# A selective scan's next chunk, prepared at other places of the loop: TensorE's fills, ScalarE's activations and one product moved

## The chip, the cores and the metric

The kernel runs on one NeuronCore of a Trainium2 chip. Five engines work side by side: TensorE (PE in the profile; its weight loads are PEld), VectorE (DVE), ScalarE (ACT), GpSimd (POOL), and SyncE (SP), which here only issues transfers. Each engine executes its own instructions in the order in which the program gives them, and semaphores tie the engines together. The metric is the device time of one execution, in microseconds (us).

## The reference, cut to what matters

Four layers are applied in turn to four images of 256 channels on 64 x 64 places: a deformable convolution, an attention layer, a second deformable layer, and a state-space layer (Mamba). The change touches the last of them alone. With `_gn` a group normalisation over 32 groups, `xs` the 4096 places of an image as a sequence, it computes

```
xz = xs @ in_proj_w.T;  u, res = split(xz)            # 512 channels each
u = silu(causal_conv4(u) + conv_b)                    # four taps per channel
dt, Bm, Cm = split(u @ x_proj_w.T)                    # 16, 16, 16
delta = softplus(dt @ dt_proj_w.T + dt_proj_b)        # 512 channels
state = exp(delta * A) * state + delta * Bm * u       # 16 states per channel, over the sequence
y = sum over states of state * Cm;  y = (y + u * D) * silu(res)
x = x + y @ out_proj_w.T
```

## The kernel before, in words

**Tiling.** Everything is float32 but the weights that repeat a row of B. The 512 channels are four blocks `dc` of 128 partitions. The sequence of an image is cut into 8 chunks of 512 places, and a chunk has 16 steps, one for each state n. So the loop in `layer3` runs over 128 steps s for each of four images; chunk j = s // 16, n = s % 16.

**One step.** TensorE repeats row n of B over all partitions into a PSUM bank, `bn` (`state`, L1460; there is one such bank). VectorE multiplies du = delta * u with it (L1537: 2048 elements per partition, or 1536 at the eight "helped" n, 14, 15 and 0 to 5, where GpSimd makes the fourth block at L1468 from a copy of the row that a transfer brought, `bs`). Then, for each of the four blocks, ScalarE makes da = exp(delta * A) (L1547, into one of two PSUM banks) and VectorE runs the scan over it (L1548). GpSimd keeps the last column (`carry`, L1560) and multiplies with the repeated row of C (L1563; `cn`, a transfer, four buffers). Two steps later TensorE adds the four blocks into PSUM with an identity matrix (`add`, L1438; called y below). `h` has four buffers. At n = 2 VectorE gates the four sums of the chunk before (`gated`, L1514).

**The preparation of the next chunk** (`front`) and the output projection of the last (`close`) are cut into small parts, and a table `slots` puts each part at a place: a step and a half. A part has up to two functions: `pe`, which issues TensorE's matmuls into the one bank `front`, and `rest`, which empties the bank by ScalarE, or does other work. `fill(s, half)` issues the first matmul part of a place ahead of time; `empty(s, half)` issues the rests, and further matmul parts. Half 0 is emptied after the second scan of a step and half 1 after the fourth; half 2 follows GpSimd's product; half -1 is ahead of the scans. The parts of chunk j > 1 begin LEAD steps ahead of their base: step 0 of `front(j)` falls on n = 16 - LEAD of chunk j - 2, that is, most of the preparation for chunk k + 1 runs during chunk k.

The parts: `begin` (two activations of 512 that normalise the chunk); four projections, P0 to P3 (L1242, each four matmul rows of the profile); four convolutions, C0 to C3 (L1285, eight rows); the silu over all blocks with a second one for the gate, and a load of an activation table ahead of each change of function; shares (dt, B, C; L1309) and their eviction; four steps of the delta projection (L1324) with two activations each; Exp, "one" (1 + exp), its complement (L1351), Ln, each an activation of 2048; three additions and one product on GpSimd; three copies in bf16 that split the rows of B exactly (`split`); four gate projections (also L1242). `close` has two output products Z0, Z1 (L1396 and L1400, ten rows each), each followed by an eviction and a transfer out; `fetch` loads the next image's chunk; `count` has VectorE's statistics of it (L152).

**What sets the order.** Under `manual_schedule` TensorE, ScalarE, VectorE and GpSimd execute in the order in which this loop is written. In step s TensorE has: the bank of half 0 (filled at the end of the step before), the fill of half 1, `bn` of step s + 1, the y of step s - 2. At each place ScalarE has the parts in the order in which they were put.

Of the kernel before, what the change touches and what calls it, by code (L numbers as in the profile page):

```python
# [9 lines left out]
F32 = mybir.dt.float32  # L10
# [6 lines left out]
P = 128  # L17
# [46 lines left out]
class Net:  # L64
# [1016 lines left out]
    def layer3(self, x, out, nxt, early):  # L1081
# [3 lines left out]

        nc, tc = self.nc, self.tc
        C = 512
        NC, LEAD = N // C, 4  # L1090
        with (
            tc.tile_pool(name="l3a", bufs=1) as pa,
            tc.tile_pool(name="l3b", bufs=2) as pb,
# [23 lines left out]
            nc.gpsimd.memset(carry, 0.0)  # L1117
            tail = pa.tile([P, 4, 3], F32, tag="tail", name="tail")
            nc.gpsimd.memset(tail, 0.0)
            kept = pa.tile([P, 2, C], F32, tag="kept", name="kept")  # L1120
            chunks = [{} for _ in range(NC)]

            def bank():
# [112 lines left out]
            def project(j, dc, to):  # L1236
                c = chunks[j]

                def pe():
                    c["b"] = bank()  # L1240
                    for ct in range(2):
                        nc.tensor.matmul(  # L1242
                            c["b"], win[:, ct, bass.ts(dc, P)], c["xn"][:, ct, :], start=(ct == 0), stop=(ct == 1)
                        )

                return pe, lambda: nc.scalar.copy(to(), c["b"])

            def gate(j, dc):
                def to():
                    if dc == 0:  # L1250
                        chunks[j]["sres"] = pb.tile([P, 4, C], F32, tag="sres", name="sres")
                    return chunks[j]["sres"][:, dc, :]

                return project(j, 4 + dc, to)
# [5 lines left out]
            def front(j):  # L1260
# [15 lines left out]
                put(0, 0, None, begin)  # L1276

                for dc in range(4):
                    put((dc + 1) // 2, (dc + 1) % 2, *project(j, dc, lambda dc=dc: c["up"][:, dc, 3:]))

                def convolve(dc):
                    def pe():
                        c["b"] = bank()
                        for i in range(4):
                            nc.tensor.matmul(  # L1285
                                c["b"], conv[:, dc, i, :], c["up"][:, dc, i : i + C], start=(i == 0), stop=(i == 3)
                            )

                    def rest():
                        nc.scalar.activation(c["u"][:, dc, :], c["b"], AF.Identity, bias=cb[:, dc : dc + 1])  # L1290
                        if dc == 0:
                            nc.gpsimd.tensor_copy(tail, c["up"][:, :, C : C + 3])

                    return pe, rest

                for dc in range(4):
                    put(2 + dc, 1, *convolve(dc))
                def silu():
                    nc.scalar.activation(c["u"], c["u"], AF.Silu)
                    gate_silu(j - 1)  # L1300
                    tables()

                put(6, 0, None, silu)

                def shares():

# [8 lines left out]
                    c["cd"] = self.dram.tile([2 * DS, C], F32, tag="cd", name="cd")  # L1315
                    nc.sync.dma_start(out=c["cd"], in_=c["dbc"][16:48, :])

                put(7, 1, shares, keep)


                def step(dc):
# [11 lines left out]
                    return pe, rest  # L1333

                for dc in range(4):
                    put(8 + dc // 2, dc % 2, *step(dc))
                put(10, 0, None, lambda: nc.scalar.activation(c["du"], c["du"], AF.Exp, scale=-1.0))

                def one():
                    c["w"] = pa.tile([P, 4, C], F32, tag="w3", name="w3")  # L1340
                    nc.scalar.activation(c["w"], c["du"], AF.Identity, bias=self.ones[:, 0:1])

                put(10, 1, None, one)


                put(10, 2, None, lambda: nc.gpsimd.tensor_add(c["delta"], c["delta"], c["du"]))
                put(
                    12,
                    0,
                    None,  # L1350
                    lambda: nc.scalar.activation(c["du"], c["w"], AF.Identity, bias=self.ones[:, 0:1], scale=-1.0),  # L1351
                )
                put(13, 0, None, lambda: nc.scalar.activation(c["w"], c["w"], AF.Ln))
                last = 17 if j > 1 else 15
                put(13, 2, None, lambda: nc.gpsimd.tensor_add(c["delta"], c["delta"], c["du"]))
                put((13 + last) // 2, 2, None, lambda: nc.gpsimd.tensor_add(c["delta"], c["delta"], c["w"]))
                put(last, 2, None, lambda: nc.gpsimd.tensor_mul(c["du"], c["delta"], c["u"]))

                for dc in range(4):
                    at = ((14, 0), (14, 1), (15, 0), (15, 1)) if j > 1 else ((10, 1), (11, 0), (11, 1), (12, 1))  # L1360
                    put(*at[dc], *gate(j, dc))
                def split(i):
                    def part():
                        if i == 0:
# [14 lines left out]
                    return part  # L1379

                for i in range(3):
                    put((11, 12, 14)[i], i % 2, None, split(i))
                return todo

            def close(j):

                c = chunks[j]
                last = j == NC - 1
                todo = []

                def project(ot):
                    def pe():
                        c["b"] = pda.tile([P, C], F32, tag="da", name="out") if last else bank()
                        c["z", ot] = c["b"]
                        for dc in range(4):
                            nc.tensor.matmul(  # L1396
                                c["b"], wo[:, dc, bass.ts(ot, P)], c["sres"][:, dc, :], start=(dc == 0), stop=False
                            )
                        xs = kept[:, ot, :] if last else x[:, ot, bass.ts(j, C)]
                        nc.tensor.matmul(c["b"], self.ident, xs, start=False, stop=True)  # L1400

                    def rest():
                        to = kept if last else x[:, :, bass.ts(j, C)]
                        nc.scalar.copy(to[:, ot, :], c["z", ot])
                        nc.sync.dma_start(out=out[ot, :, bass.ts(j, C)], in_=to[:, ot, :])

                    return pe, rest

                for ot in range(2):
                    todo.append((11 + 2 * ot - LEAD, 1, *project(ot)))  # L1410
                if not last:
                    todo.append((15 - LEAD, -1, None, lambda: fetch(j)))

                    todo.append((13 - LEAD + DS if j < NC - 2 else 17 - LEAD, -1, None, lambda: count(j)))
                return todo

            def fetch(j):
# [7 lines left out]
                        self.note(x, ct, j)  # L1425

            def keep():
                for ct in range(2):
                    nc.scalar.copy(kept[:, ct, :], x[:, ct, bass.ts(NC - 1, C)])

# [30 lines left out]

            def quarter(s):

                if s < NC * DS:
                    c = chunks[s // DS]
                    hs[s] = pb.tile([P, 4, C], F32, tag="h", name="h", bufs=4)
                    if s % DS in helped:
                        nc.gpsimd.tensor_mul(hs[s][:, 3:4, :], c["du"][:, 3:4, :], c.pop(("bs", s % DS)))  # L1468


            slots = {}
            for j in range(1, NC):
                for step, half, pe, rest in front(j):
                    at = DS * (j - 1) - (LEAD if j > 1 else 2) + step
                    if at >= 0:
                        slots.setdefault((at, half), []).append((pe, rest))
            for j in range(NC - 1):
# [7 lines left out]
            for i in range(2):  # L1485

                def gates(i=i):
                    c = chunks[0]
                    if i == 0:
                        c["sres"] = pb.tile([P, 4, C], F32, tag="sres", name="sres")  # L1490
                    for dc in (2 * i, 2 * i + 1):
                        nc.scalar.copy(c["sres"][:, dc, :], c["gates"][dc])

                slots.setdefault((i, 0), []).append((None, gates))

            def fill(at, half):

# [18 lines left out]
            with tc.manual_schedule(  # L1516
# [15 lines left out]
                for s in range(total):  # L1532
                    j, n = s // DS, s % DS
                    c = chunks[j]
                    h = hs.pop(s)
                    d = 3 if n in helped else 4
                    nc.vector.tensor_mul(  # L1537
                        h[:, :d, :], c["du"][:, :d, :], c.pop(("bn", n)).to_broadcast([P, d, C])
                    )
                    ahead(s + 2)  # L1540
                    empty(s, -1)
                    if j and n == 2:
# [2 lines left out]
                    def scan(dc):  # L1545
                        da = pda.tile([P, C], F32, tag="da", name="da")
                        nc.scalar.activation(da, c["delta"][:, dc, :], AF.Exp, scale=al[:, dc, n : n + 1])  # L1547
                        nc.vector.tensor_tensor_scan(  # L1548
                            h[:, dc, :], da, h[:, dc, :], carry[:, dc, n : n + 1], ALU.mult, ALU.add
                        )  # L1550

                    scan(0)
                    scan(1)
                    quarter(s + 1)
                    empty(s, 0)
                    fill(s, 1)
                    scan(2)
# [7 lines left out]
                        nc.vector.tensor_mul(h[:, 0:2, :], h[:, 0:2, :], cn.to_broadcast([P, 2, C]))  # L1565
                        nc.gpsimd.tensor_mul(h[:, 2:4, :], h[:, 2:4, :], cn.to_broadcast([P, 2, C]))
                    empty(s, 2)
                    state(s + 1)
                    late.append((j, n, h))
                    if len(late) > 2:  # L1570
                        add(*late.pop(0))
# [131 lines left out]
```

## Time and profile before

| | |
|---|---|
| runs, median (lowest to highest), us | 9831.43 (9831.18 to 9837.31) |
| profiled execution, us | 9825.3 |
| its span, us | 9823.5 |
| first product with B of a chunk 0 to the last of chunk 7, images 0 to 3, us | 929.8, 929.8, 930.2, 921.8 |
| four scans (L1548), mean of one, ns | 1264 (x2048) |
| product with B (L1537), mean, ns | 1998 (x512, two forms) |
| product with C (L1563), mean, ns | 4527 (x508) |
| da (L1547), mean, ns | 689 (x2048) |

A row of the profile is a group of equal instructions: source line, engine, operation, output and inputs by the program's names, count, busy time, mean of one. In a timeline a row begins with its start and length in us, and the brackets at its end say how long the engine was idle before it and whose result ended that. A row of a table by stretches gives the stretch, its length, then each engine's busy time in the order of its heading (PE, PEld, DVE, ACT, POOL), TensorE's granted clock, the share of the transfer engines and GB/s.

An instruction's length is not its pitch: two scans start 1.18 us apart though each is 1.26 long, and two f32 matmul rows 0.43 apart though each is 0.59 long.

### The profile page before, as it was taken

The numbers are of one execution on the slowest core, as the hardware profiler recorded it, in microseconds if no ns is written. First come the engines' busy times: TensorE is split into PE (matmuls) and PEld (weight loads), VectorE is DVE, ScalarE is ACT, GpSimd is POOL, SyncE is SP. The second block draws the span as 40 slices with busy tenths as digits, with TensorE's granted clock in tenths as the row PEclk, the third lists the DMA queues.
The fourth block names the chain that finished last, engine by engine and source line by source line (L and its number), as shares of the span: only waits on it lengthen the run. The fifth ranks groups of instructions, "written<-read, shape, count | busy, mean of one in ns | idle before, by whom it ended". The sixth has DMA issues, their size and how long they took to land. (4 is left out here: it accounts for less than half of the span.)

```text
span 9823.5 us, 89566 instructions
## 1 busy us (share of the span) xinstructions
PE 8552.6 (87%) x29129; PEld 4208.7 (43%) x29129; DVE 7522.1 (77%) x8175; ACT 4893.9 (50%) x7532; POOL 7112.0 (72%) x4220
## 2 busy tenths in 40 slices
PE   5789998998778999899878899989987889998997
PEld 3643343333464344333346434433334643443333
DVE  4764498999676459899968645989996764689998
ACT  3753335665474333566547433266655733326664
POOL 3746687888474668798857467789985746778997
PEclk9999999999899999999989999999998999999999
DMA  7840011222783001122279201122228820111221
GB/s 255 319 158 1 26 50 56 64 62 67 257 320 139 1 30 47 58 63 63 67 272 333 107 1 35 51 57 62 62 64 313 324 73 1 39 51 55 60 60 51
DMA packets 415274, 1024.78 MB, mean 104 GB/s; under 512 B 38771, under 2 KB 111916, under 8 KB 412748
## 3 DMA queue, kind: packets, MB, share of 16 engines
q0 software_dynamic: 165888, 604.05, 17.0%
q1 hardware_dynamic: 248908, 414.90, 13.7%
q8 instruction: 233, 3.82, 0.2%
q14 instruction: 245, 2.01, 0.1%
HBM read 851.70 MB, written 93.37 MB: 96 GB/s over the span
## 5 line engine op out<-in xcount | busy, mean ns | idle before, releaser
L1548 DVE TENSOR_TENSOR_SCAN h<-da,carry,h 128x512 f32<-128x512 f32 x2048 | 2469.0, 1264 | 138.3 <-ACT da L1547 78.0
L1563 POOL TENSOR_TENSOR h<-h,cn 128x2048 f32<-128x2048 f32 x508 | 2299.7, 4527 | 41.3 <-POOL carry L1560 0.8
L1547 ACT ACTIVATE da<-delta,l3a 128x512 f32<-128x512 f32 x2048 | 1393.1, 689 | 1064.1 <-DVE h L1548 1061.5
L1438 PE MATMUL y<-h,ident 128*128 128x512 f32 x4096 | 1907.6, 610 | 12.4 <-POOL h L1563 12.4
L344 POOL DMA_INDIRECT g<-tab,idx x1152 | 1359.8, 1180 | 748.6 <-issue 367.5
L565 POOL TENSOR_TENSOR acc<-acc,e 128x1024 f32<-128x1024 f32 x480 | 1126.0, 2346 | 539.5 <-ACT e L561 517.6
L388 PE MATMUL pz<-cols,l0w 128*128 128x256 f32 x4608 | 1211.3, 409 | 184.6 <-DVE cols L377 73.9
L1438 PEld LDWEIGHTS y<-h,ident 128*128 128x128 f32 x4096 | 801.7, 196 | 1251.6 <-issue 1166.7
L353 DVE SCALAR_TENSOR_TENSOR r<-g,wx,r 128x512 f32<-128x512 f32 x1152 | 858.4, 745 | 373.4 <-ACT r L352 251.4
L462 DVE TENSOR_REDUCE m<-pm 128x3 f32<-128x1536 f32 (+2 forms) x340 | 599.5, 1763 | 699.9 <-PE pm L452 699.9
L1537 DVE TENSOR_TENSOR h<-du,bn 128x2048 f32<-128x2048 f32 (+1 forms) x512 | 1022.8, 1998 | 49.9 <-PE bn L1460 49.8
L388 PEld LDWEIGHTS pz<-cols,l0w 128*128 128x128 f32 x4608 | 893.2, 204 | 353.7 <-DVE cols L377 110.4
L561 ACT ACTIVATE e<-sc 128x1024 f32<-128x1024 f32 x512 | 496.1, 1020 | 1029.5 <-PE sc L548 1029.5
L572 PE MATMUL cx<-e,v 128*128 128x512 f32 x2048 | 1001.0, 616 | 0.0
L845 DVE TENSOR_TENSOR prod<-ring,A 128x1280 f32<-128x1280 f32 x640 | 922.4, 1480 | 77.9 <-DMA ring<-ring 60.2
L352 ACT ACTIVATE r<-g,wx 128x512 f32<-128x512 f32 x1152 | 826.5, 717 | 265.0 <-DMA g<-tab,idx 211.6
L862 PE MATMUL pacc<-prod,ident 128*128 128x512 f32 x1920 | 914.5, 611 | 32.8 <-DVE prod L845 21.8
L854 POOL TENSOR_TENSOR prod<-prod 128x512 f32<-128x512 f32 x640 | 801.2, 1277 | 182.2 <-DVE prod L845 157.3
L370 PE MATMUL pt<-ident,acc 128*128 128x128 f32 x2304 | 428.3, 293 | 295.0 <-DVE acc L361 234.2
L572 PEld LDWEIGHTS cx<-e,v 128*128 128x128 f32 x2048 | 352.4, 189 | 599.3 <-issue 596.8
L360 ACT ACTIVATE acc<-r,wy 128x256 f32<-128x256 f32 x1152 | 571.3, 496 | 16.5 <-DVE r L353 13.7
L361 DVE SCALAR_TENSOR_TENSOR acc<-r,wy,acc 128x256 f32<-128x256 f32 x1152 | 548.6, 477 | 0.0
(255 smaller groups left out, 10767.4 us busy)
## 6 DMA issues: line engine op xcount, KB each, us to landing
cn<-cd SPq DMA_DIRECT2D x512, 256.0 KB
tab<-vt SPq DMA_DIRECT2D x112, 640.0 KB
bs<-cd SPq DMA_DIRECT2D x256, 256.0 KB
ring<-ring SPq DMA_DIRECT2D x288, 126.0 KB
ring<-ring SPq DMA_DIRECT2D x288, 124.0 KB
g<-tab,idx POOLq DMA_INDIRECT x1152
x<-in_x SPq DMA_DIRECT2D x64, 256.0 KB
out<-x SPq DMA_DIRECT2D x56, 256.0 KB
```

Source lines behind the costliest of these rows:

```text
L344: nc.gpsimd.indirect_dma_start(out=g[:], out_offset=None, in_=tab[:, :], in_offset=bass.IndirectOffsetOnAxis(ap=idx[:, t, k : k + 1], axis=0),
L353: nc.vector.scalar_tensor_tensor(r, g[:, :, 1, :], wx[:, 1, t, k : k + 1], r, ALU.mult, ALU.add)
L388: nc.tensor.matmul(sums[m][:, ot, :256], wf[:, i, bass.ts(ot, P)], cols[m][:, i, :], start=(i == 0), stop=(i == 17),)
L565: nc.gpsimd.tensor_add(b["acc"], b["acc"], e)
L572: nc.tensor.matmul(blocks[qb]["cx"], v[:, 4 * (i + kt // 4 * 4) + kt % 4, :], e[:, bass.ts(i % 2, 512)], start=(kt == 0 and i == 0), stop= ...
L845: nc.vector.tensor_mul(d["prod"][:, :, t, :].rearrange("p x (g c) -> p x g c", c=GC), ring[y // VR % 4][:, :, y % VR, :].rearrange("p x (g ...
L862: nc.tensor.matmul(d["pd"], self.ident, prod[:, wx, :], start=(wy == 0 and wx == 4), stop=(wy == WIN - 1 and wx == 2),)
L1438: nc.tensor.matmul(c["ys"][dc], self.ident, h[:, dc, :], start=False, stop=(n == DS - 1))
L1537: nc.vector.tensor_mul(h[:, :d, :], c["du"][:, :d, :], c.pop(("bn", n)).to_broadcast([P, d, C]))
L1547: nc.scalar.activation(da, c["delta"][:, dc, :], AF.Exp, scale=al[:, dc, n : n + 1])
L1548: nc.vector.tensor_tensor_scan(h[:, dc, :], da, h[:, dc, :], carry[:, dc, n : n + 1], ALU.mult, ALU.add)
L1563: nc.gpsimd.tensor_mul(h, h, cn.to_broadcast([P, 4, C]))
```

## The change

LEAD is 5 instead of 4, and the parts are put at other places. For a steady chunk, by n of the chunk during which they run (".1" is half 1):

| part | before | after |
|---|---|---|
| begin | 12.0 | 11.0 |
| P0, P1, P2, P3 | 12.1, 13.0, 13.1, 14.0 | 11.1, 12.0, 12.1, 15.1 |
| C0, C1, C2, C3 | 14.1, 15.1, 0.1, 1.1 | 13.1, 14.1, 0.1, 1.1 |
| silu with the gate's | 2.0 | 2.0 |
| shares; delta's four | 3.1; 4.0 to 5.1 | the same |
| split 0, 1, 2 | 7.0, 8.1, 10.0 | 6.0, 7.0, 10.0 |
| Exp, one, complement, Ln | 6.0, 6.1, 8.0, 9.0 | 6.0, 7.0, 8.1, 9.1 |
| GpSimd's four | 6.2, 9.2, 11.2, 13.2 | the same |
| gates 0 to 3 | 10.0, 10.1, 11.0, 11.1 | 9.0, 9.1, 10.0, 10.1 |
| Z0, Z1 | 7.1, 9.1 | 6.1, 8.1 |
| fetch; count of two chunks back | 11; 9, ahead of the scans | 10; 2.0 |

At each place the part with matmuls now comes first, so its bank is emptied ahead of other activations there. `bn` of step s + 1 is issued in the middle of step s, ahead of the fill of half 1, and no longer after everything but y. In the steps listed in `visits` (where the silu is: n = 2, and step 4 of chunk 0) the product of the next step is issued between scans 1 and 2. GpSimd's helping product has a buffer of its own, `hq`, from which the fourth scan reads. `kept` shares the buffer of `xn3`. Chunk 1, whose first parts run ahead of the loop, has its own places.

```diff
-        NC, LEAD = N // C, 4
+        NC, LEAD = N // C, 5
...
                 for dc in range(4):
-                    put((dc + 1) // 2, (dc + 1) % 2, *project(j, dc, lambda dc=dc: c["up"][:, dc, 3:]))
+                    at = ((0, 1), (1, 0), (1, 1), (4, 1))[dc]
+                    put(*at, *project(j, dc, lambda dc=dc: c["up"][:, dc, 3:]))
...
                 for dc in range(4):
-                    put(2 + dc, 1, *convolve(dc))
+                    at = ((2, 1) if j > 1 else (3, 0), (3, 1), (5, 1), (6, 1))[dc]
+                    put(*at, *convolve(dc))
...
-                put(6, 0, None, silu)
+                put(7, 0, None, silu)
+                visits.append(DS * (j - 1) + (2 if j > 1 else 4))
...
-                put(7, 1, shares, keep)
+                put(8, 1, shares, keep)
...
-                    put(8 + dc // 2, dc % 2, *step(dc))
-                put(10, 0, None, lambda: nc.scalar.activation(c["du"], c["du"], AF.Exp, scale=-1.0))
...
+                    put(9 + dc // 2, dc % 2, *step(dc))
...
                 for i in range(3):
-                    put((11, 12, 14)[i], i % 2, None, split(i))
+                    put((11, 12, 15)[i], 0, None, split(i))
+
+                put(11, 0, None, lambda: nc.scalar.activation(c["du"], c["du"], AF.Exp, scale=-1.0))
...
+                put(12, 0, None, one)
...
+                put(
+                    13,
+                    1,
+                    None,
+                    lambda: nc.scalar.activation(c["du"], c["w"], AF.Identity, bias=self.ones[:, 0:1], scale=-1.0),
+                )
+                put(14, 1, None, lambda: nc.scalar.activation(c["w"], c["w"], AF.Ln))
+                last = 18 if j > 1 else 16
...
-                    todo.append((11 + 2 * ot - LEAD, 1, *project(ot)))
+                    todo.append((6 + 2 * ot, 1, *project(ot)))
...
-                if s < NC * DS:
+                if s < NC * DS and s % DS in helped:
                     c = chunks[s // DS]
-                    hs[s] = pb.tile([P, 4, C], F32, tag="h", name="h", bufs=4)
-                    if s % DS in helped:
-                        nc.gpsimd.tensor_mul(hs[s][:, 3:4, :], c["du"][:, 3:4, :], c.pop(("bs", s % DS)))
+                    hq = hs[s, 3] = pb.tile([P, C], F32, tag="hq", name="hq")
+                    nc.gpsimd.tensor_mul(hq, c["du"][:, 3, :], c.pop(("bs", s % DS))[:, 0, :])
+
+            def product(s):
+
+                if s not in hs:
+                    c, n = chunks[s // DS], s % DS
+                    h = hs[s] = pb.tile([P, 4, C], F32, tag="h", name="h", bufs=4)
+                    d = 3 if n in helped else 4
+                    nc.vector.tensor_mul(h[:, :d, :], c["du"][:, :d, :], c.pop(("bn", n)).to_broadcast([P, d, C]))
...
+            for todo in slots.values():
+                todo.sort(key=lambda part: part[0] is None)
...
                     scan(0)
                     scan(1)
                     quarter(s + 1)
+                    state(s + 1)
+                    if s in visits:
+                        product(s + 1)
                     empty(s, 0)
                     fill(s, 1)
...
                     empty(s, 2)
-                    state(s + 1)
```

More of the change, by code (lines that the diff above doesn't have):

```diff
@@ L1119, in layer3 @@
             nc.gpsimd.memset(tail, 0.0)
-            kept = pa.tile([P, 2, C], F32, tag="kept", name="kept")
             chunks = [{} for _ in range(NC)]
@@ L1290, in rest @@
                         nc.scalar.activation(c["u"][:, dc, :], c["b"], AF.Identity, bias=cb[:, dc : dc + 1])
-                        if dc == 0:
+                        if dc == 2:
                             nc.gpsimd.tensor_copy(tail, c["up"][:, :, C : C + 3])
@@ L1335, in front @@
                 for dc in range(4):
-                    put(8 + dc // 2, dc % 2, *step(dc))
-                put(10, 0, None, lambda: nc.scalar.activation(c["du"], c["du"], AF.Exp, scale=-1.0))
[L1339 to L1361, printed above, removed]
+                    put(9 + dc // 2, dc % 2, *step(dc))
                 def split(i):
@@ L1381, in front, with one @@
                 for i in range(3):
-                    put((11, 12, 14)[i], i % 2, None, split(i))
+                    put((11, 12, 15)[i], 0, None, split(i))
+                put(11, 0, None, lambda: nc.scalar.activation(c["du"], c["du"], AF.Exp, scale=-1.0))
+                def one():
+                    c["w"] = pa.tile([P, 4, C], F32, tag="w3", name="w3")
+                    nc.scalar.activation(c["w"], c["du"], AF.Identity, bias=self.ones[:, 0:1])
+                put(12, 0, None, one)
+                put(11, 2, None, lambda: nc.gpsimd.tensor_add(c["delta"], c["delta"], c["du"]))
+                put(
[6 more added lines that the diff above has]
+                last = 18 if j > 1 else 16
+                put(14, 2, None, lambda: nc.gpsimd.tensor_add(c["delta"], c["delta"], c["du"]))
+                put((14 + last) // 2, 2, None, lambda: nc.gpsimd.tensor_add(c["delta"], c["delta"], c["w"]))
+                put(last, 2, None, lambda: nc.gpsimd.tensor_mul(c["du"], c["delta"], c["u"]))
+                for dc in range(4):
+                    at = ((14, 0), (14, 1), (15, 0), (15, 1)) if j > 1 else ((11, 1), (12, 0), (12, 1), (13, 1))
+                    put(*at[dc], *gate(j, dc))
                 return todo
@@ L1398, in pe @@
                             )
-                        xs = kept[:, ot, :] if last else x[:, ot, bass.ts(j, C)]
+                        xs = c["kept"][:, ot, :] if last else x[:, ot, bass.ts(j, C)]
                         nc.tensor.matmul(c["b"], self.ident, xs, start=False, stop=True)
                     def rest():
-                        to = kept if last else x[:, :, bass.ts(j, C)]
+                        to = c["kept"] if last else x[:, :, bass.ts(j, C)]
                         nc.scalar.copy(to[:, ot, :], c["z", ot])
@@ L1409, in close @@
                 for ot in range(2):
-                    todo.append((11 + 2 * ot - LEAD, 1, *project(ot)))
+                    todo.append((6 + 2 * ot, 1, *project(ot)))
                 if not last:
-                    todo.append((15 - LEAD, -1, None, lambda: fetch(j)))
-                    todo.append((13 - LEAD + DS if j < NC - 2 else 17 - LEAD, -1, None, lambda: count(j)))
+                    todo.append((10, -1, None, lambda: fetch(j)))
+                    todo.append((2 + DS, 0, None, lambda: count(j)) if j < NC - 2 else (13, -1, None, lambda: count(j)))
                 return todo
@@ L1427, in keep @@
             def keep():
+                kept = chunks[-1]["kept"] = pa.tile([P, 2, C], F32, tag="xn3", name="kept")
                 for ct in range(2):
@@ L1462, in quarter @@
             def quarter(s):
-                if s < NC * DS:
+                if s < NC * DS and s % DS in helped:
                     c = chunks[s // DS]
-                    hs[s] = pb.tile([P, 4, C], F32, tag="h", name="h", bufs=4)
-                    if s % DS in helped:
-                        nc.gpsimd.tensor_mul(hs[s][:, 3:4, :], c["du"][:, 3:4, :], c.pop(("bs", s % DS)))
+                    hq = hs[s, 3] = pb.tile([P, C], F32, tag="hq", name="hq")
[6 more added lines that the diff above has]
+                    nc.vector.tensor_mul(h[:, :d, :], c["du"][:, :d, :], c.pop(("bn", n)).to_broadcast([P, d, C]))
             slots = {}
+            visits = [DS * (NC - 1) + 2]
             for j in range(1, NC):
                 for step, half, pe, rest in front(j):
-                    at = DS * (j - 1) - (LEAD if j > 1 else 2) + step
+                    at = DS * (j - 1) - (LEAD if j > 1 else 3) + step
                     if at >= 0:
@@ L1534, in layer3 @@
                     c = chunks[j]
[L1535 to L1539, printed above, removed]
+                    product(s)
+                    h = hs[s]
                     ahead(s + 2)
@@ L1547, in scan @@
                         nc.scalar.activation(da, c["delta"][:, dc, :], AF.Exp, scale=al[:, dc, n : n + 1])
+                        hb = hs.pop((s, dc), h[:, dc, :])
                         nc.vector.tensor_tensor_scan(
-                            h[:, dc, :], da, h[:, dc, :], carry[:, dc, n : n + 1], ALU.mult, ALU.add
+                            h[:, dc, :], da, hb, carry[:, dc, n : n + 1], ALU.mult, ALU.add
                         )
```

## The prediction

> **What bounds the kernel now.** The change touches layer 3 alone, so I read the engines' busy time first, then the stretches of one steady chunk of layer 3, then who waits there.
>
> ```profile
> PE 8552.6 (87%) x29129; PEld 4208.7 (43%) x29129; DVE 7522.1 (77%) x8175; ACT 4893.9 (50%) x7532; POOL 7112.0 (72%) x4220
> ```
>
> No engine fills the span. The next view gives busy time in image 0's chunk 3, cut at the starts of the product with B (L1537): steps 0-1, 2, 3-5, 6-7, 8-10, 11-13, 14-15.
>
> ```profile
> 1916.28:1930.45 14.17, 14.17 (x35) 6.26 (x34) 13.12 (x10) 6.53 (x11) 14.01 (x8) 1.00 0.28 76
> 1930.45:1941.55 11.10, 11.10 (x27) 4.85 (x26) 8.88 (x9) 9.94 (x10) 7.04 (x4) 1.00 0.36 94
> ...
> 1975.39:1998.00 22.61, 19.62 (x43) 8.49 (x43) 22.23 (x19) 15.35 (x20) 21.03 (x10) 0.92 0.23 70
> ...
> 2019.20:2034.09 14.89, 14.12 (x35) 6.12 (x34) 13.20 (x12) 6.04 (x10) 14.73 (x9) 1.00 0.24 70
> sum 117.81, PE 108.34 PEld 46.45 DVE 111.65 ACT 74.26 POOL 105.80; mean PE 15.48 PEld 6.64 DVE 15.95 ACT 10.61 POOL 15.11
> ```
>
> VectorE (DVE) is busy 111.65 of 117.81 us, with TensorE (PE) and GpSimd close behind. A step without a wait takes 6.55 us where GpSimd helps (n = 14, 15, 0 to 5: 1.82 for the product, four scans at 1.18), else 7.09 (2.36 and the same scans). The four gating products add 2.2 at n = 2: 8 x 6.55 + 8 x 7.09 + 2.2 = 111.3 without any wait. Steady chunks take 117.5 or 117.8, of which 1.0 is L152's statistics at n = 9. So about 5.3 is idle per chunk. Where:
>
> ```profile
> 1939.18 2.46 DVE L1548 TENSOR_TENSOR_SCAN h<-da,carry,h 128x512 f32<-128x512 f32 x2 [2.21 <-ACT da L1547]
> ...
> 2027.01 1.75 DVE L1537 TENSOR_TENSOR h<-du,bn 128x1536 f32<-128x1536 f32 x1 [0.99 <-PE bn L1460]
> 2034.09 1.75 DVE L1537 TENSOR_TENSOR h<-du,bn 128x1536 f32<-128x1536 f32 x1 [0.42 <-PE bn L1460]
> ```
>
> The timeline of DVE shows 2.3 at n = 2 (ScalarE makes no da during the silu), 0.9 to 1.2 after n = 14 and 0.5 after each of 15, 0 and 1 (bn late: the step takes PE's 7.08); n = 8 adds 0.3. TensorE's own timeline, n = 6 to 9, then a later one:
>
> ```profile
> 1963.53 0.38 PE L1460 MATMUL bn<-bp,pickn 128*128 128x512 bf16 x1 [1.48 <-DVE h L1537]
> 1963.74 3.59 PE L1438 MATMUL y<-h,ident 128*128 128x512 f32 x8
> 1967.17 3.60 PE L1396 MATMUL front<-sres,l3b 128*128 128x512 f32 x8
> ...
> 1977.71 0.43 PE L1460 MATMUL bn<-bp,pickn 128*128 128x512 bf16 x1 [2.43 <-DVE h L1537]
> 1977.93 5.29 PE L1438 MATMUL y<-h,ident 128*128 128x512 f32 x8
> 1983.05 3.60 PE L1396 MATMUL front<-sres,l3b 128*128 128x512 f32 x8
> ...
> 2367.54 0.59 PE L1460 MATMUL bn<-bp,pickn 128*128 128x512 bf16 x1 [3.28 <-DVE h L1537]
> 2367.92 4.85 PE L1438 MATMUL y<-h,ident 128*128 128x512 f32 x8
> ```
>
> Two things matter. bn(n+1) cannot start until the product of step n has read the one bn bank (end of product + 0.05, about 2.31 into a step). Today the output products (L1396) start before that wait and run through it. And after a long idle TensorE is slow for a while: eight matmuls take 5.29 or 4.85 instead of 3.6.
>
> **What the Trainium skill says.** "TensorE: Matmul & The Clock Gate", Part 1, says the clock halves after an idle window of about 3.4 us and recovers after a busy one. Here it happened after every one of eleven 3.28 us gaps (1.2 to 2.7 us lost, 1.76 on average), and after about half of the 2.43 ones, so the trace is harsher. Part 2 of that page says matmuls stay in program order; the waits above agree. "ScalarE: Activation LUTs", What ACT_TABLE_LOAD costs, gives 1283 ns a load, as the rows show (1.28), but its extra drain of 1.38 us is not in this trace: the next activation follows within 0.02.
>
> **The change, part by part.** Times count from the product's start of the step named. Durations: f32 matmul pair 0.86 (two rows 0.43 apart), so C (convolution) 3.43, projection or gate 1.72, output Z 4.29, y 3.43; bn 0.22; evictions 0.59 (next starts 0.5 to 0.6 later); da 0.61 apart; 2048-wide activations 1.85 to 1.9; bt/bp copies 0.61. PE's result reaches ScalarE 0.16 after its last row's pitch.
>
> Gains:
> 1. The silu (still n = 2). DVE now does product(3), 1.82, between scans 1 and 2. da2 is ready near 8.55, and scan 2 would start at 8.3, with the two statistics (L152, moved from n = 9) at 9.3. Steps 2+3 take 16.4 instead of 17.65, and n = 9 loses 1.0: -2.25. Where there are no statistics (chunk 1, image 3) -2.0.
> 2. Projections and convolutions start a step earlier, one bank filling at a time. PE has 7.07 (bn, C, y) at n = 14, 0 and 1, 5.36 at 15, 27 over four steps against DVE's 26.2; its lag stays within the 1.5 us a C may be late before da0 is. bn now comes before C, so it is never late. 14, 15, 0, 1 go from 28.9 (28.7 or 29.0) to 26.4 (0.2 kept: GpSimd's hq(15) ends at 5.5, wanted at 5.37): -2.5.
> 3. n = 8's wait of 1.57 for GpSimd (L1351) goes, since that activation moves half a step: -0.3.
>
> Losses, all from bn standing before the fill of half 1:
> 4. n = 6: Z0 starts at 2.53, not when PE is free, ends at 6.98, evicted 7.0 to 7.6; da0(7), da1(7) follow until T7+1.7. Then n = 7 holds both copies (1.22) and "one" (1.9) ahead of da2, ready at 5.5; scan 2 wants it at 4.74: +0.8. (n = 6's copies and Exp fit by about 0.2.)
> 5. n = 8: no fill at n = 7, so PE is idle from y's end, T7+6.97, to T8+2.31: 3.3 us, which the trace shows ends in half rate. At full rate Z1 ends at 6.98, its eviction stands ahead of the 1.9 us activation (bank first), da0(9) ends at 10.2, and scan 0 wants it at 7.09+2.36 = 9.45: +0.8. Half rate adds the 1.76 of the eleven gaps, taken as 1.7: +2.5.
> 6. n = 9 (full rate; half rate moves all of it alike): after Z1 at T8+6.82 come y to 10.25 and gate 0 to 11.97, read at 12.13 = T9+5.05. Its eviction precedes da2, done at T9+6.25, while the scans, begun at 3.15, want it at 5.5: +0.8.
> 7. n = 10: gate 1 waits for gate 0's eviction and ends at T9+7.4, y at 10.9, gate 2 is read at 12.7 = T10+4.1 (T10 = T9+8.65). Its eviction and the third copy precede da2, ready at 6.05 instead of 4.74: +1.3. At n = 11 y ends at 1.5, ahead of bn's 2.31: PE has caught up.
> Sum of losses 5.4, of gains 5.05: a steady chunk 118.0 with statistics (mean before 117.65), 117.2 in image 3 (before 116.85): +0.35 each.
>
> Hidden at no cost: hq's own buffer and kept in xn3's place (GpSimd's 1.27 and ScalarE's copies are unchanged); the outputs' DMAs and fetches one step earlier on SP's queue, behind which cn's loads wait, but these have four buffers. Uncovered, a late cn would hold GpSimd's 4.53 product and then y; in layer 3's waits no GpSimd row waits for cn.
>
> Other chunks. Chunk 0 (no Z, silu without gating): product(5) in the silu and an earlier C3 take steps 3 to 5 down by 3.1; n = 9 has an eviction, two copies and "one" before da2 (+1.5); its 2.6 us wait at n = 15 is GpSimd's queue of additions, which stays (-0.2): -1.8. Chunk 1: before it had n = 0, 1 free, so gains 3.5 (or 2.2 in images 2 and 3): 117.3, against 115.8 or 114.6: +1.5 and +2.7. Chunk 6: n = 14, 15 free already: +1.8, +2.0 in image 3. Chunk 7 has no preparation: 0.
>
> Sum: 4 x -1.8 = -7; chunk 1, 2 x 1.5 + 2 x 2.7 = +8.4; chunks 2 to 5, 16 x 0.35 = +5.6; chunk 6, 3 x 1.8 + 2 = +7.4. Total +14 on the profiled execution's 9825.3 (span 9823.5), so 9839; the runs' median, 9831.43, lies 6 higher, so the forecast is 9846.
>
> **Rivals.**
> (a) TensorE keeps full rate at n = 8: 24 chunks (six in each of four images) less 1.7, so 41 less: 9805. For: a 2.43 gap kept it half the time. Against: 11 of 11 gaps of 3.28.
> (b) The new stalls don't come, because TensorE runs ahead or ScalarE isn't late: the gains alone, 4 x 3.3 (chunk 0) + 4 x 2.9 + 16 x 5.05 + 4 x 3.6 = 120, so 9831 - 120 = 9711. Against: bn's bank is single, and the waits for L1537 in the trace are just that.
> (c) Slower: the lag that starts at n = 8 doesn't end at n = 11. If gate 3 and the first projection are still late at 12, ScalarE's begin (1.6) and evictions hold da2 once or twice more at 0.8: 24 x 1.6 = 38 more, 9884. It decides once PE comes out of n = 10 over 0.8 us later than step 7 has it (1.5 against 2.31).
> (d) The gain at 14 to 1 is only half, since GpSimd (14.73 of 14.89 busy there) becomes the bound: +1.1 in 16 chunks, 9864.
>
> **How the numbers follow.** Forecast 0.5 (its own range 9822 to 9872), (a) 0.17, (b) 0.06, (c) 0.15, (d) 0.12. Half the chance lies in a sum of opposite terms of 5 each, so an error of 1 us a chunk is 24 us over the 24 chunks; the range 9797 to 9888 takes in (a) and (c) and leaves out (b). Within 0.2% (about 20 us, what a measurement can tell from no change) is 9812 to 9851. The forecast gives it 0.25, slower 0.22, faster 0.03; (a) gives faster 0.12, same 0.05; (b) faster; (c) and (d) slower 0.25, same 0.02. Faster 0.21, same 0.32, slower 0.47.
>
> **What would show it.** In the profile after: at n = 2 no wait of DVE for da over 0.4; at 15, 0, 1 steps of 6.55 and no wait for bn; waits of DVE for da at n = 7, 9 (twice) and 10 of about 0.8, 2.5, 0.8 and 1.3; a PE gap of about 3.3 before bn at n = 8, with slow rows after it. Wrong if n = 9 holds no wait, or if waits appear at 11 to 13.

## The result and the profile after

The changed kernel takes 9883.12 us (median of five runs, 9880.86 to 9888.44), the kernel before 9832.65 (five runs); the ratio is 1.0049, 95% interval 1.0036 to 1.0062. It is 50 us slower, inside the forecast range, on the side that held the most chance, and 37 above the forecast of 9846.

Everything new lies in layer 3. I measure it as the time from the first product with B of an image to its last (the starts of that row in the timeline), summed over the four images ("the loops" below): 3711.7 us before, 3761.7 after, +50.0. The later comparisons use this sum too, because the kernel before itself took 9850 and 9864 us when it was timed beside the experiments; ratios are always against its runs of the same occasion.

The stretches of chunk 3 of image 0 after the change, cut at the same steps as the table in the prediction but for two cuts (steps 2 and 3 together, as the product of step 3 now lies inside step 2; then 4 and 5). Columns as there.

```profile
1911.29:1924.40 13.11, 13.11 (x33) 5.78 (x32) 12.90 (x11) 5.74 (x9) 12.95 (x8) 1.00 0.36 91
1924.40:1940.82 16.42, 16.42 (x40) 7.25 (x40) 16.41 (x18) 13.00 (x15) 14.04 (x7) 1.00 0.24 68
...
1969.04:1995.06 26.02, 22.79 (x50) 9.72 (x50) 21.17 (x17) 14.91 (x20) 20.39 (x9) 0.93 0.16 56
...
2016.32:2029.43 13.11, 13.11 (x33) 5.77 (x32) 12.90 (x11) 6.83 (x11) 12.95 (x7) 1.00 0.22 67
sum 118.14, PE 108.78 PEld 46.47 DVE 111.33 ACT 73.95 POOL 105.37; mean PE 15.54 PEld 6.64 DVE 15.90 ACT 10.56 POOL 15.05
```

The gains are there: steps 0 and 1 take 13.11 instead of 14.17, steps 14 and 15 13.11 instead of 14.89, and in steps 2 and 3 VectorE is busy for 16.41 of 16.42 us. Steps 8 to 10 gave it back: 26.02 instead of 22.61, although the statistics (1.0) left them. The timeline of VectorE, n = 7 to 10, shows the waits by size and place:

```profile
1966.66 2.46 DVE L1565 TENSOR_TENSOR_SCAN h<-da,carry,h 128x512 f32<-128x512 f32 x2 [0.81 <-ACT da L1563]
...
1980.85 2.46 DVE L1565 TENSOR_TENSOR_SCAN h<-da,carry,h 128x512 f32<-128x512 f32 x2 [2.47 <-ACT da L1563]
1984.11 2.46 DVE L1565 TENSOR_TENSOR_SCAN h<-da,carry,h 128x512 f32<-128x512 f32 x2 [0.80 <-ACT da L1563]
...
1992.68 2.46 DVE L1565 TENSOR_TENSOR_SCAN h<-da,carry,h 128x512 f32<-128x512 f32 x2 [1.37 <-ACT da L1563]
```

That is 0.81, 2.47, 0.80 and 1.37 us for da, at n = 7, 9 (twice) and 10; the prediction had 0.8, 2.5, 0.8 and 1.3. TensorE's timeline of the same stretch shows why:

```profile
1956.25 0.38 PE L1467 MATMUL bn<-bp,pickn 128*128 128x512 bf16 x1 [1.08 <-DVE h L1482]
1956.46 3.59 PE L1402 MATMUL front<-sres,l3b 128*128 128x512 f32 x8
...
1971.35 0.38 PE L1467 MATMUL bn<-bp,pickn 128*128 128x512 bf16 x1 [3.35 <-DVE h L1482]
1971.56 5.29 PE L1402 MATMUL front<-sres,l3b 128*128 128x512 f32 x8
...
1980.98 1.88 PE L1242 MATMUL front<-xn,l3a 128*128 128x512 f32 x4
```

bn stands first and waits for the product of its step, and only then come Z0 and Z1; in step 8 TensorE had been idle for 3.35 us ahead of bn, and Z1's first eight rows took 5.29 us instead of 3.59.

By chunk, summed over the four images (us):

| | chunk 0 | 1 | 2 to 5 | 6 | 7 | all |
|---|---|---|---|---|---|---|
| before | 479.2 | 460.8 | 1879.2 | 463.2 | 429.2 | 3711.7 |
| after | 493.9 | 478.9 | 1884.0 | 472.4 | 432.6 | 3761.7 |
| difference | +14.7 | +18.1 | +4.8 | +9.2 | +3.4 | +50.0 |
| predicted | -7 | +8.4 | +5.6 | +7.4 | 0 | +14 |

So the steady chunks came as worked out, and 31 of the 36 us missed are in the first two chunks of each image.

### The profile page after: what moved, and what is told of

Its sections match the earlier page's. It is cut to its first block, busy times and chain, and to the rows that moved or that the text cites. A ratio compares the mean times of both kernels' runs of the same rounds, so it can differ in the third digit from the quotient of the medians.

```text
span 9886.6 us, 89300 instructions
## 1 busy us (share of the span) xinstructions
PE 8599.2 (87%) x29129; PEld 4237.1 (43%) x29129; DVE 7518.2 (76%) x8175; ACT 4885.1 (49%) x7532; POOL 7110.3 (72%) x4220
## 3 DMA queue, kind: packets, MB, share of 16 engines
q1 hardware_dynamic: 248908, 414.90, 13.2%
## 5 line engine op out<-in xcount | busy, mean ns | idle before, releaser
L1565 DVE TENSOR_TENSOR_SCAN h<-da,carry,h 128x512 f32<-128x512 f32 x1792 | 2172.8, 1265 | 223.1 <-ACT da L1563 177.5
L1445 PE MATMUL y<-h,ident 128*128 128x512 f32 x4096 | 1882.0, 603 | 10.9 <-POOL h L1583 10.9
```

The costliest lines, as they stand in the source:

```text
L1445: nc.tensor.matmul(c["ys"][dc], self.ident, h[:, dc, :], start=False, stop=(n == DS - 1))
L1565: nc.vector.tensor_tensor_scan(h[:, dc, :], da, hb, carry[:, dc, n : n + 1], ALU.mult, ALU.add)
```

## The experiments

The theory is that bn's place on TensorE, ahead of the fill of half 1, makes the losses, with the half rate after idle time as an amplifier. The rivals are ScalarE's new places and the bank-first order, or a bound elsewhere that takes back any gain. Sums of the loops are of the profiled execution of each.

**bn late again.** The gains' places stay; bn goes back to the end of the step except where the product in the silu needs it.

```diff
-                    state(s + 1)
                     if s in visits:
+                        state(s + 1)
                         product(s + 1)
...
                     empty(s, 2)
+                    if s not in visits:
+                        state(s + 1)
```

> The changed kernel, but the repeat of B's next row (bn) is issued at the end of a step again, as before the change, except in the steps with the silu. Theory (bn ahead of the fill of half 1 holds TensorE until the product of the step is done): the waits for da at n = 7 and 9 go (steps of 7.09 instead of 8.01 and 10 to 11.6), that at n = 10 shrinks to 1.0 or less, chunk 0's late silu goes too; about 4 us in each of 24 chunks and 25 to 35 in chunks 0 and 1, so 9735 to 9790, best guess 9755. Rival (the places of ScalarE's activations and the bank-first order are to blame, wherever bn stands): 9870 or more. If bn late costs again at n = 14 to 1 as before the change, 0.5 a step there takes back up to 2 us a chunk: 9800.

Measured: 9754.89 us, ratio 0.9892 (0.9875 to 0.9908); loops 3607.7, 154 below the changed kernel and 104 below the kernel before. A chunk from 2 to 5 takes 112.6. TensorE's timeline at n = 6 to 9 of chunk 3, image 0, in this run:

```profile
1955.39 3.60 PE L1402 MATMUL front<-sres,l3b 128*128 128x512 f32 x8
1958.82 1.02 PE L1406 MATMUL front<-x,ident 128*128 128x512 f32 x2
1959.68 0.38 PE L1467 MATMUL bn<-bp,pickn 128*128 128x512 bf16 x1
...
1963.85 0.38 PE L1467 MATMUL bn<-bp,pickn 128*128 128x512 bf16 x1 [0.36 <-DVE h L1482]
...
1967.50 3.60 PE L1402 MATMUL front<-sres,l3b 128*128 128x512 f32 x8
```

Z0 now starts 0.9 us into step 6 (the step begins at 1954.45) instead of 2.5, Z1 ahead of step 8, and the only wait left at bn in this stretch is 0.36. Steps 7, 9 and 10 average 7.12, 7.09 and 7.30 us in chunks 2 to 6, where the changed kernel has 8.01, 10.16 and 8.57. Steps 14, 15, 0 and 1 stay at 6.56 to 6.58: bn at the end of a step is in time there, so the gain at these steps came from the places of projections and convolutions, not from bn. The rival of the places on ScalarE falls: they are the same here. That the time met the best guess of 9755 is in part luck, since the kernel before took 17 us more beside this run (9849.75) than in the result above.

**Only those five steps.** The changed kernel, bn late at n = 6 to 10 of chunks 1 to 7 alone.

```diff
-                    state(s + 1)
+                    soon = s in visits or not (j > 0 and n in (6, 7, 8, 9, 10))
+                    if soon:
+                        state(s + 1)
...
                     empty(s, 2)
+                    if not soon:
+                        state(s + 1)
```

> The changed kernel with bn late at n = 6 to 10 of chunks 1 to 7 alone. Theory (steps 4 to 7 of the prediction: every loss in the steady chunks comes from bn ahead of Z0, Z1 and the gates at these five steps): chunks 2 to 6 fall to 112.7 each as in e1, from 117.8, the four chunks 1 by about 5 each; chunk 0 stays at 493 in sum. Rival (part of it comes from bn's place at other steps, or from lag that is carried in from them): 114 or more.

One execution: 9767.14 us beside 9842.96 for the kernel before; loops 3632.5. Chunks 2 to 6 average 112.6 each, chunk 1 falls from 119.7 to 114.5, chunk 0 stays (493.8 in sum), and chunk 7 falls to 429.4 in sum, where the kernel before has 429.2. All of the steady chunks' loss comes from bn's place in five steps; nothing is carried in from elsewhere.

**The half rate by itself.** The changed kernel with matmuls that nobody reads in the idle stretch at n = 7.

```diff
                 put(8, 1, shares, keep)
+                def warm():
+                    b = bank()
+                    for i in range(4):
+                        nc.tensor.matmul(b, conv[:, 0, i, :], c["u"][:, 0, :], start=(i == 0), stop=(i == 3))
+                if j > 1:
+                    put(12, 1, warm, lambda: None)
```

> The changed kernel with one idle group of four matmuls (3.4 us, written into the front bank and read by nobody) in half 1 of n = 7, where TensorE idles for 3.3 us ahead of bn at n = 8. Theory (the idle makes the next matmuls run at half rate, which puts 1.7 us into Z1 and so into n = 9): steps at n = 9 of 8.7 in all chunks instead of 10.0 to 11.6, 24 x 1.8 us less: 9840 (9828 to 9855). Rival (the clock isn't the cause; the length of n = 9 comes from the order alone): no change or slower, 9880 to 9900, as TensorE has 3.4 us more to do.

Measured: 9866.05, ratio 1.0015 (1.0006 to 1.0023), against the changed kernel's 1.0049: a third of a per cent, some 33 us; loops 3726.5, 35 less. Z1 of chunk 3 in this run:

```profile
1975.81 0.38 PE L1475 MATMUL bn<-bp,pickn 128*128 128x512 bf16 x1
1976.03 3.59 PE L1410 MATMUL front<-sres,l3b 128*128 128x512 f32 x8
```

No idle time before bn, and eight rows take 3.59 again. Step 9 is 8.66 or 8.67 in 23 of 24 chunks (1 to 6 of each image) and 8.31 in one, where the changed kernel had 8.3 to 8.7 in 5 of 24 chunks, 10.0 to 10.4 in 15 and 11.5 to 11.6 in 4. So the idle time costs 1.5 us a chunk on average, and more work on TensorE makes the kernel faster.

**The order on ScalarE.** The changed kernel without the sort.

```diff
-            for todo in slots.values():
-                todo.sort(key=lambda part: part[0] is None)
```

> The changed kernel without the sort that puts the part with matmuls first at each place: at n = 8 the long activation runs while Z1 is still on TensorE, at n = 10 the third copy runs before gate 2's eviction. Theory (step 5 and 7 of the prediction: the eviction ahead of the activation adds the activation's 1.9 us to a late bank): n = 9 falls from 10.4 to about 8.4, n = 10 from 8.57 to about 8.0, chunk 0's n = 9 by 2; 9813 (9795 to 9835). Rival (only bn's place on TensorE counts): within 15 us of the changed kernel, 9870 to 9885.

Measured: 9875.74, ratio 1.0028 (1.0019 to 1.0036); loops 3737.8, 24 less. That is short of the expected 70, the time lies in the rival's range, and here a step of my theory fell. VectorE's timeline, n = 8 to 10 of chunk 3:

```profile
1989.87 2.46 DVE L1563 TENSOR_TENSOR_SCAN h<-da,carry,h 128x512 f32<-128x512 f32 x2 [1.47 <-ACT da L1561]
...
1997.80 2.46 DVE L1563 TENSOR_TENSOR_SCAN h<-da,carry,h 128x512 f32<-128x512 f32 x2 [0.73 <-ACT da L1561]
```

n = 10 gained as expected (0.73 instead of 1.37). At n = 9 the wait in front of scan 0 is gone, but scan 2 waits 1.47 instead of 0.80: in this full-rate chunk the step takes 8.66, as it does bank-first (8.66 in the run with the unread matmuls); its mean over chunks 2 to 6 is 10.06 against 10.16. The two waits of step 9 were one. Gate 0 reaches the bank at a time that TensorE's order sets, and da2 stands behind its eviction whatever scan 0 did. Of the 24 us, 15 are n = 10 and 7 chunk 0.

**The product amid the silu alone,** on the kernel before (the product as a function of its own, and the list `visits`, are left out of the cut).

```diff
...
                     quarter(s + 1)
+                    if s in visits:
+                        state(s + 1)
+                        product(s + 1)
                     empty(s, 0)
...
                     empty(s, 2)
-                    state(s + 1)
+                    if s not in visits:
+                        state(s + 1)
```

> The kernel before with one edit: in the steps with the silu bn and the product of the next step come between scans 1 and 2. Theory (gain 1 of the prediction is worth what it says): 2.3 us in 24 chunks, 2.6 in chunk 0 of each image, less up to 0.8 in a chunk where TensorE is then late for delta's first step at n = 4: 9768 to 9790. Rival (TensorE, busy 108 of 117.6 us, becomes the bound and the time comes back at n = 4 or at 14 to 1): 9820 to 9835.

Measured: 9824.19, ratio 0.9973 (0.9963 to 0.9983), 27 us; loops 3676.8, 35 less. Half of what was expected, and in time inside the rival's range. Steps 2 and 3 of chunks 2 to 6 take 15.8 instead of 17.65, but 4 and 5 take 6.97 and 6.99 instead of 6.55:

```profile
1941.34 2.46 DVE L1553 TENSOR_TENSOR_SCAN h<-da,carry,h 128x512 f32<-128x512 f32 x2 [0.31 <-ACT da L1552]
...
1948.33 2.46 DVE L1553 TENSOR_TENSOR_SCAN h<-da,carry,h 128x512 f32<-128x512 f32 x2 [0.33 <-ACT da L1552]
```

VectorE is ready earlier, and now delta's steps on TensorE are late for ScalarE. The rival was right in part: 0.85 of 1.85 us a chunk came back at n = 4 and 5. Chunk 0 keeps more, 1.9 us each: 471.7 in sum, where the kernel before has 479.2.

**bn early at the convolutions alone,** else late. Against the changed kernel:

```diff
-                    state(s + 1)
+                    soon = s in visits or n in (13, 14, 15, 0, 1)
+                    if soon:
+                        state(s + 1)
...
                     empty(s, 2)
+                    if not soon:
+                        state(s + 1)
```

> The run with bn late everywhere (e1) but for n = 13, 14, 15, 0 and 1, where the convolutions run: there bn is issued ahead of them, as in the changed kernel. Theory (bn ahead of the convolutions gives nothing, since with their new places bn is in time at the end of a step too, and in chunks 0 and 1 it is what makes the convolutions late after an idle TensorE): steady chunks 112.6 as in e1, n = 1 of chunk 1 back at 7.3 to 8.0 and chunk 0 at 122 to 124; layer 3's four loops 15 to 30 us above e1. Rival (gain 2 of the prediction, bn must stand ahead of C to be in time): below e1 by 10 us or more. Second rival (bn's place costs in steady chunks wherever it is early): 24 x 1 us or more above e1 in chunks 2 to 6.

Measured: 9768.16, ratio 0.9904 (0.9887 to 0.9920); loops 3615.2, 7.5 above the run with bn late, less than the 15 to 30 expected. Chunk 1 is 8.5 worse in sum (n = 1 at 6.77, n = 2 at 7.46), as the theory says; chunk 0 is not (476.2 against 478.9), since its held convolutions lie at n = 2 and 3, which this edit left late. Steady chunks don't move (0.1 each). Early bn at the convolutions gives nothing in the steady chunks and costs in chunk 1.

**bn late in chunk 0 alone,** else as in the changed kernel.

```diff
-                    state(s + 1)
+                    soon = s in visits or not (j == 0)
+                    if soon:
+                        state(s + 1)
...
                     empty(s, 2)
+                    if not soon:
+                        state(s + 1)
```

> The changed kernel with bn late in chunk 0 of each image alone (but for its silu step). Theory (the part that the prediction missed, +22 us in the four chunks 0, is the third and fourth convolution held behind bn and run at half rate after idle time, which sends the silu late): the four chunks 0 sum to about 479 as in e1 instead of 493.9, chunks 2 to 7 stay as in the changed kernel. Rival (chunk 0 loses by the new places alone, or because GpSimd's queue holds it until n = 15 whatever comes before): 490 or more.

One execution: 9885.14 beside 9842.96; loops 3746.8. The chunks 0 sum to 479.8 instead of 493.9 (9 of these 14 us at steps 3 to 5, 5 at step 9), and chunks 2 to 7 still to 2790.5 (2789.0 in the changed kernel). TensorE and then VectorE in chunk 0 of image 1 of the changed kernel, n = 1 to 5:

```profile
4010.26 0.59 PE L1467 MATMUL bn<-bp,pickn 128*128 128x512 bf16 x1 [2.50 <-DVE h L1482]
4010.64 3.29 PE L1242 MATMUL front<-xn,l3a 128*128 128x512 f32 x4
4016.82 0.56 PE L1467 MATMUL bn<-bp,pickn 128*128 128x512 bf16 x1 [2.89 <-DVE h L1482]
4017.18 5.15 PE L1286 MATMUL front<-up,conv 128*128 128x512 f32 x8
...
4029.03 0.38 PE L1467 MATMUL bn<-bp,pickn 128*128 128x512 bf16 x1
4029.25 3.60 PE L1286 MATMUL front<-up,conv 128*128 128x512 f32 x8
```

```profile
4034.18 2.46 DVE L1565 TENSOR_TENSOR_SCAN h<-da,carry,h 128x512 f32<-128x512 f32 x2 [2.98 <-ACT da L1563]
...
4041.82 1.28 DVE L1565 TENSOR_TENSOR_SCAN h<-da,carry,h 128x512 f32<-128x512 f32 x1 [3.54 <-ACT da L1563]
```

TensorE is at half rate from the wait of 2.50 us on: the projection's four rows take 3.29 where 1.88 is usual. The third convolution is held behind bn for 2.89 us more and still runs at half rate, the two y groups and bn follow, and the fourth convolution (4029.25) ends 3.4 us into step 4. Its eviction holds all of step 4's da, and the silu behind it step 5's.

**Chunk 1's old places,** on the run with bn late.

```diff
-                    at = ((0, 1), (1, 0), (1, 1), (4, 1))[dc]
+                    at = ((0, 1), (1, 0), (1, 1), (4, 1) if j > 1 else (3, 0))[dc]
...
-                    at = ((2, 1) if j > 1 else (3, 0), (3, 1), (5, 1), (6, 1))[dc]
+                    at = ((2, 1), (3, 1), (5, 1), (6, 1))[dc] if j > 1 else (3 + dc, 1)
```

> e1 with the convolutions of chunk 1 at the places they had before the change (the fourth projection in half 0 of step 0, the convolutions in half 1 of steps 0 to 3). Theory (in chunk 0 the third convolution now waits for the projection ahead of it and starts after 3.3 us of an idle TensorE, at half rate, so that the silu comes 2 us late): chunk 0 falls from 120.7 to about 118.5, four times 2 us: 8 us below e1. Rival (chunk 0's loss comes from the queue of GpSimd or from the silu's own place): the same as e1 within 2 us in the loops.

Measured: 9765.99, ratio 0.9899 (0.9883 to 0.9916), the same as with bn late; loops 3601.7, 6 less, of which chunk 0 has 4.5 (118.6 each in place of 119.7; step 3 falls from 8.95 to 7.86). About half of the expected 8 us, by the cause that was expected: in chunk 0 of image 1 the third convolution takes 3.70 us after an idle TensorE of 2.64, where with bn late it took 5.40 after 3.33. The rest of chunk 0 varies at n = 12, where ScalarE waits for a projection, and at n = 15, where VectorE waits for GpSimd's hq.

**Unsorted on top of that.** The same two lines removed.

> e7 without the sort that puts the part with matmuls first. Theory (with bn late the banks are full in time, so their order on ScalarE matters only in chunk 0, at n = 9 and 12): 1.5 us less in each chunk 0 and 0.2 in each steady one at n = 10, 10 us below e7. Rival (bank first is needed at 8 to 13, since a late eviction holds TensorE): 10 us or more above e7.

Measured: 9771.07, ratio 0.9904 (0.9888 to 0.9921); loops 3609.1, 7 above. Step 10 is 7.57 instead of 7.29 in the steady chunks; chunk 0 gains at n = 12 (7.09 instead of 9.20) and loses as much at n = 15 (10.45 instead of 8.73), where GpSimd's queue sets the end. With bn late, bank first is worth 0.3 us a chunk: the rival's side.

Four versions beat both kernels by 1% or more and cannot be told apart in time: bn late, bn early at the convolutions alone, bn late with chunk 1's old places, and the last one. The third has the shortest loops.

## Why the prediction was right and where it was wrong

**The sign and the mechanism were right.** The rivals (a) and (b), faster, fell: TensorE did run at half rate in 19 of 24 chunks, and the stalls came. Rivals (c) and (d) fell as well: in chunks 2 to 6 steps 11 to 13 average 7.09 to 7.11, so the lag ended at n = 11, and 14, 15, 0 and 1 took 26.2 together. That the measured time lies 1 us from (c)'s 9884 is chance.

**Steps 1 to 3 (gains)** held: 16.42 for steps 2 and 3 where 16.4 was predicted, 26.2 for 14 to 1 where 26.4 was, 7.11 at n = 8. But the reason given in step 2, that bn ahead of C is never late, was not what did it: with bn at the end of the step these steps are as short. The new places did it: these four steps hold three convolutions instead of four. And step 1 taken alone, on the old places, is worth 1.0 us a chunk, 0.85 less than what it shows at n = 2 and 3; in the changed kernel TensorE is on time for delta, presumably because the projections and convolutions lie earlier.

**Steps 4 to 7 (losses)** held in place and in sum: +0.92 at n = 7 (0.8 predicted), +3.07 at n = 9 on average (3.3), +1.48 at n = 10 (1.3); a chunk from 2 to 6 took 118.0 with statistics, as predicted, and 117.1 in image 3 (117.2). Step 5's split was wrong, though. It charged the eviction ahead of the long activation with 0.8 us, and step 6 added 0.8 more; without that order the step was as long, since gate 0's arrival alone sets it. The half rate was 1.5 rather than 1.7 on average, a mean of no loss and of losses up to 2.9; that it came near the forecast owes something to luck (see the last section).

**The step that failed is "Other chunks".** For chunk 0 it counted the product in the silu and "an earlier C3" as 3.1 us off steps 3 to 5, with no term for bn ahead of the convolutions, and forecast -1.8 a chunk; it was +3.7. Steps 3 to 5 took 27.4 us where the kernel before took 25.1 and the forecast had 22.0. In chunk 0 bn also holds the convolutions, next to the extra y of the first step, and TensorE is at half rate after idle time; the silu began 5.3 us into step 4. bn late in chunk 0 alone takes back 14 of the 15 us. The loss at n = 9 came in the size forecast (1.6 for 1.5), but 1.15 of it goes with bn late, so it is not ScalarE's order alone. What then still lacks to the forecast of 472 is in part chunk 1's new places, worth 4.5 us in sum. The runs with bn late there come to 474 to 480, and only the product in the silu on the old places reached the forecast (471.7).

For chunk 1 the forecast was +8.4 in sum (its own terms, 5.4 of losses less gains of 3.5 or 2.2, would give about +10) and +18.1 was measured. Its loss at n = 6 to 10 is 5.3 a chunk, as predicted (the run with these steps late gives back 21 in sum). The rest begins at n = 1 and 2: VectorE's wait for hq at the end of chunk 0 (3.4 us, 2.6 before the change), which I had seen, leaves TensorE idle for 3.5 us and its convolutions at half rate behind bn. bn early at the convolutions alone costs 8.5 us here; how much of this is the half rate was not measured apart. I counted the wait and not what it does to TensorE.

For chunk 7 nothing was forecast, as it has no preparation, and +3.4 was measured, in step 7 of two images above all. It still has Z0 and Z1 of the chunk before: with bn late at n = 6 to 10 step 7 is back at 7.09 and the four chunks sum to 429.4, so this is the same loss.

One small slip in the sum of the steady chunks changes nothing: without statistics step 1 gives 2.0, so image 3 should have had +0.6 a chunk and not +0.35.

**The hidden edits** (hq's own buffer, kept in xn3's place, transfers a step earlier) were not tested one by one. All of them are in the run with bn late, whose steady chunks in image 0 are at 112.6 where 112.3 is VectorE's own work with the statistics, so together they cost at most 0.3 us in a steady chunk.

"TensorE: Matmul & The Clock Gate", Part 1, of the Trainium skill bore out as a mechanism: idle time, then half the rate. Its 3.4 us window is no safe limit here: the kernel before slowed after 10 of 25 gaps of 2.43 at n = 8, and 3.35 us was not always enough, with 19 of 24.

## What to carry to other kernels

An instruction's place in an engine's queue counts by what it waits for, more than by what it costs: bn takes 0.22 us, and put ahead of work that didn't depend on VectorE it tied TensorE to VectorE's step and turned a gain of 104 us in layer 3 into a loss of 50. When several edits come together, work each engine's queue through step by step, and do so for the first and last rounds of the loop apart, where parts meet other neighbours than in the steady ones. Ahead of a long stretch of matmuls, look for the idle time that slows it; filling that with matmuls that nobody needs was worth a third of a per cent.

## What the hardware showed that I had not expected

After the same idle time of 3.35 us TensorE lost 0 us in 5 chunks of 24, about 1.3 to 1.7 in 15 and 2.9 in 4, in one and the same execution. In the kernel before, eleven gaps of 3.28 had all lost 1.2 us or more, but the changed kernel has fifteen gaps of 3.28 ahead of bn at full rate, in chunks 6 and 7, and eight of them lost nothing. So eleven of eleven was no rule, and the prediction leaned on it against rival (a): the length of the gap alone does not tell whether TensorE slows.
